# An LSTM with residual on one core: half products of x in two column quarters at 256 columns, and recurrent products that begin with the other two

## The chip, the cores and the metric

One core of a Trainium2 chip runs the whole program. The metric is the device time of one execution in microseconds. The kernel before was timed three times: 3061.52, 3061.62 and 3063.40 us, so its median is 3061.62 us.

## The reference

The input x has 32 sequences of 512 steps with 512 features; the start state h0 is given, the cell state starts at zero, and all numbers are 32-bit floats. The result is x plus the hidden states of an LSTM with 512 units. Cut to what is computed:

```python
xW = jnp.einsum('ntd,dg->ntg', x, Wx) + b          # Wx: 512 x 2048
def step(carry, xw_t):
    prev_h, prev_c = carry
    a = xw_t + prev_h @ Wh                         # Wh: 512 x 2048
    i = jax.nn.sigmoid(a[:, :Hd])
    f = jax.nn.sigmoid(a[:, Hd:2 * Hd])
    o = jax.nn.sigmoid(a[:, 2 * Hd:3 * Hd])
    g = jnp.tanh(a[:, 3 * Hd:])
    next_c = f * prev_c + i * g
    next_h = o * jnp.tanh(next_c)
    return ((next_h, next_c), next_h)
(_, _), hs = jax.lax.scan(step, (h0, c0), jnp.swapaxes(xW, 0, 1))
x = x + jnp.swapaxes(hs, 0, 1)
```

There are two kinds of product: x times Wx, which hangs on nothing but the inputs, and in each of the 512 steps the state times Wh, which hangs on the step before.

## The kernel before, in words

**Quarters.** Both kinds of product are issued as matmuls with 32 columns of weights, so that one matmul uses one quarter of the array's 128 columns. The quarter j of a matmul is named by the partitions that it writes, 32j to 32j+31. Four matmuls, one for each quarter, make one set.

**The recurrent product.** `h_part(t)` (L552) issues 16 matmuls: for each quarter k of the 512 units of the state, and for each column quarter j, 512 columns of `wh_sb`. They add into `bank_of(t)`, one of the two tiles `gbank`, which ScalarE filled before with x's part of that step (`seed_step`, L1035, a copy from `xw`). `cell(t)` (L565) then goes: sigmoids and tanh on ScalarE from `gbank` into `s` and `o`, products and a sum on VectorE (`prod`, `s`), a tanh on ScalarE (`tanh_c`), the product `hbuf`, and a transpose in two halves into `ht`, the weights of `h_part(t + 1)`. The first half of `ht` holds k = 0 and 1, the second k = 2 and 3.

**The products of x.** From step 18 to step 497 x times Wx is made in 15 groups of 32 steps by a scheme with fewer multiplications: 26 products for each group (a `slot` counts them through, 390 in all), and each of them out of seven of half the size (r = 1 to 7). One such (slot, r) is called an item here. An item is one set: four matmuls, one for each quarter, with 256 columns (`HW`) of the right operand in `vring` (L906). The left operand is a sum of blocks of x (`ubuf`), or a block in `xs` or `r`; the result goes to one of five `xbank` or to half of `bbank`. `evacuate` (L946) takes finished items to SBUF.

**Where they stand.** In the main loop `h_part(t)` is issued first, then `emit_matmuls(n)` (L868) issues n quarters of an item's work, then `cell(t)` is recorded. So between two recurrent products TensorE has items to do while the cell runs. `pos[0]` counts quarters of items. The count that is due by a step is worked out at L1588 as `R * 7 * 4 + (t + i - STREAM0) * R * 7 * 2 // GS * 2` with R = 26 and GS = 32, which grows by 22 or 24 a step, 22.75 in the mean. Where an item doesn't fit, a half of it is issued (`size = 2`): the half with q = 0 at the end of a step, and the half with q = 2 at the beginning of the next. In the kernel before, a half is 128 of the 256 columns in all four quarters.

Over 16 steps the formula gives, for where a step's items begin and end (0: whole, 2: in the middle of an item): five steps 0 to 2, three steps 2 to 2, five steps 2 to 0 and three steps 0 to 0. The steps 0 to 2 and 2 to 0 hold five and a half items, the other two kinds six. The main loop has 28 such rounds, so 140, 84, 140 and 84 steps.

**What sets the order.** The class `Plan` (L105) records every instruction and orders them by a model of their costs. TensorE's instructions keep the order in which they were recorded; those of the other queues are sorted by due times that are worked back from TensorE's. As everything is issued from one helper, all lines of the profile read L125, and groups are told apart by tiles.

Of the kernel before, what the change touches and what calls it, by code (L numbers as in the profile page):

```python
# [14 lines left out]
B = 32  # L15
T = 512
NJ = 4
# [5 lines left out]
HW = G * H  # L23
# [50 lines left out]
BIAS_OF = {  # L74
    2: "b1", 5: "b1-b0", 9: "-b2", 10: "b1", 12: "b0-b3", 13: "b0-b3", 14: "-b2", 15: "b3", 19: "b0-b1+b2", 21: "b3",
    22: "b0-b3",
}
# [3 lines left out]
RIGHT = {1: 0, 5: 1, 3: 2, 6: 3, 2: 4, 7: 5, 4: 6}  # L81
# [306 lines left out]
def kernel(  # L388
# [150 lines left out]
    def is_split(t):  # L539
        return t >= SPLIT  # L540

    def bank_of(t):
        return {2: xbank[3], 3: xbank[4], 4: xbank[0]}.get(t, gbank[t % 2])

    def half_of(t, i):
        if t == T - 1:
            return LAST[i][:, 0:HW]
        if is_split(t):
            return PAIRS[(t - SPLIT) % 2][i][:, 0:HW]
        return bank_of(t)[:, i * HW : (i + 1) * HW]  # L550

    def h_part(t):  # L552
        if is_split(t):
            order = [(i, k) for i, ks in ((0, (0, 1)), (1, (0,)), (0, (2, 3)), (1, (1, 2, 3))) for k in ks]
        else:
            order = [(None, k) for k in range(NJ)]
        for i, k in order:
            dst = bank_of(t) if i is None else half_of(t, i)
            m = wh_sb[:, k] if i is None else wh_sb[:, k, :, i * HW : (i + 1) * HW]
            for j in range(NJ):  # L560
                nc.tensor.matmul(
                    dst[j * B : (j + 1) * B], state["ht"][:, k], m[:, j], start=False, stop=True, skip_group_check=True
                )
# [104 lines left out]
    def group(g):  # L668
        if g not in groups:
            groups[g] = Group(g)  # L670
        return groups[g]
# [143 lines left out]
    def left_of(gr, s, r):  # L815
        b = u_block(gr, U_OF[s])
        return ubuf[:, gr.u[U_OF[s]], LEFT[r]] if b is None else b[:, 1 + LEFT[r]]

    def left_done(gr, s):
        u_used(gr, U_OF[s])  # L820
# [43 lines left out]
    pos = [0]  # L864
# [3 lines left out]
    def emit_matmuls(n):  # L868

        while n > 0 and pos[0] < 4 * len(items):  # L870
            i, q = divmod(pos[0], 4)
            row, slot, r = items[i]
            gr, s = group(slot // R), slot % R
            xb = xbank[slot % 5]
            if q == 0 and any(f in finished for f in needs(slot, r)):
                if wait_at_end[0]:
                    return
                evacuate()
            if r == 2:
                dst = bbank[:, slot % 2 * HW : (slot % 2 + 1) * HW]  # L880
            elif r in (5, 3):
                dst = xb[:, HW:W]
            else:
                dst = xb[:, 0:HW]
            start = q == 0 and (r == 2 or (r == 1 and s not in BIAS_OF))
            size = 4 if q == 0 and n >= 4 else 2
            cols = slice(q * HW // 4, (q + size) * HW // 4)
            for j in range(4):
                nc.tensor.matmul(
                    dst[j * B : (j + 1) * B, cols],  # L890
                    left_of(gr, s, r)[:, j * B : (j + 1) * B],
                    right_of(row, slot, RIGHT[r])[:, cols],
                    start=start,
                    stop=True,
                    skip_group_check=True,
                )
            pos[0] += size
            n -= size
            if pos[0] % 4 == 0:
                finished.append((slot, r))  # L900
                if r == 4:
                    left_done(gr, s)
                    if slot < HELD:
                        (free_u if slot == 1 else free_c).extend({1: (6, 7), 2: (V_OF[2],), 3: (V_OF[3],)}.get(slot, ()))

    def right_of(row, slot, k):  # L906
        if slot >= HELD:
            return vring[:, row % 3, k]
        return v_parts(V_OF[slot])[2] if k == 6 else v_parts(V_OF[slot])[k % 2][:, k // 2]

    def needs(slot, r):
        if r == 1:
            return ((slot - 5, 4),)
        if r == 2:
            return ((slot - 2, 2),)
        return {5: (), 6: ((slot, 5),), 3: ((slot, 5),), 7: ((slot, 3),), 4: ((slot, 7),)}[r]
# [29 lines left out]
    def evacuate():  # L946
        while wqueue and len(free_c) < sum(r == 5 for _, r in finished):
            w_op(True)
        for slot, r in finished:
            gr, s = group(slot // R), slot % R  # L950
            xb = xbank[slot % 5]
            if r == 5:
                gr.have[s, "c"] = take(free_c)
                t = buf_of(gr.have[s, "c"])
                nc.scalar.copy(t[:, 0:4:3], xb.rearrange("p (n c) -> p n c", n=2))
                continue
            if r in (1, 6):
                continue
            t = buf_of(gr.have[s, "c"])
            if r == 2:  # L960
                add(t[:, 0], bbank[:, slot % 2 * HW : (slot % 2 + 1) * HW], t[:, 0])
                room["dve"] -= cost_dve(256)
            elif r == 3:
                nc.scalar.copy(t[:, 1], xb[:, 0:HW])
                add(t[:, 1], xb[:, HW:W], t[:, 1])
                room["dve"] -= cost_dve(256)
            elif r == 7:
                add(t[:, 3], xb[:, 0:HW], t[:, 3])
                room["dve"] -= cost_dve(256)
            else:  # L970
                nc.scalar.copy(t[:, 2], xb[:, 0:HW])
                gr.have[s] = gr.have.pop((s, "c"))
                ready(gr, s)
        finished.clear()
# [92 lines left out]
    def v_parts(i):  # L1067
        if i < 8:
            return r1[:, i, 1:4], r2[:, i, 0:3], r2[:, i, 3]
        return split_parts(vroom[vt[i]])  # L1070
# [312 lines left out]
    with tc.manual_schedule():  # L1383
# [32 lines left out]
        for n in range(2):  # L1416
            for j in range(NJ):
# [4 lines left out]
                    start=True,  # L1422
# [44 lines left out]
        for t in range(T):  # L1467
            if t == 20:
                nc.flush()
            h_part(t)  # L1470
            for f in stores + kept_stores:
                f()
# [12 lines left out]
            if HEAD + 4 <= t < HEAD + 4 + 3 * len(V_DIRECT):  # L1485
                s, d = divmod(t - HEAD - 4, 3)
# [15 lines left out]
            if t < HEAD_STEPS:  # L1502
# [22 lines left out]
                for i, (kind, m, cs) in enumerate(chunks):  # L1525
# [16 lines left out]
                    else:  # L1542
# [22 lines left out]
                        if i == 0 and t + 1 in SEEDED and t + 1 != HEAD:  # L1565
                            seed_step(t + 1)
                        emit_matmuls(m)
                        room["dve"] += m * PROD / 4
                        if i == late_cell:
# [38 lines left out]
            if t in LATE:  # L1608
                late_loads.pop(0)()
            emit_matmuls(n)  # L1610
            load_v_ahead()
            if t == SPLIT - 1:
# [60 lines left out]
```

## Time and profile before

| what | value |
|---|---|
| median of three runs | 3061.62 us |
| the profiled execution: time | 3061.49 us |
| the profiled execution: span from first to last instruction | 3059.5 us |
| TensorE busy | 3050.5 us, 100% |
| VectorE busy | 2362.7 us, 77% |
| ScalarE busy | 1475.6 us, 48% |
| GpSimd busy | 227.7 us, 7% |
| DMA, mean | 247 GB/s |
| granted TensorE clock | 1.000 |

The profile's page is of one execution. Durations of matmuls in it are modelled ends of pipelined work, so one matmul lasts longer there than the distance to the next one that takes its place; distances between starts are the better measure. Each matmul of the program leaves two records: 466 recurrent products of 16 matmuls stand as 14,912 records.

### The profile page before, as it was taken

The numbers are of one execution on the slowest core, as the hardware profiler recorded it, in microseconds if no ns is written. First come the engines' busy times: TensorE is split into PE (matmuls) and PEld (weight loads), VectorE is DVE, ScalarE is ACT, GpSimd is POOL, SyncE is SP. The second block draws the span as 40 slices with busy tenths as digits, with TensorE's granted clock in tenths as the row PEclk, the third lists the DMA queues.
The fourth block names the chain that finished last, engine by engine and source line by source line (L and its number), as shares of the span: only waits on it lengthen the run. The fifth ranks groups of instructions, "written<-read, shape, count | busy, mean of one in ns | idle before, by whom it ended". The sixth has DMA issues, their size and how long they took to land.

```text
span 3059.5 us, 107940 instructions
## 1 busy us (share of the span) xinstructions
PE 3050.5 (100%) x43464; PEld 1586.6 (52%) x43464; DVE 2362.7 (77%) x6510; ACT 1475.6 (48%) x5499; POOL 227.7 (7%) x476
## 2 busy tenths in 40 slices
PE   9999999999999999999999999999999999999999
PEld 6644444444445555555555555555555555555666
DVE  8678787787877878788787877878778787787755
ACT  1345445454444544445445454454544545444454
POOL 1000000000000000000000000000000000000000
PEclk9999999999999999999999999999999999999999
DMA  9988887787877878778787787877877777788630
GB/s 329 326 285 279 267 254 258 239 260 242 262 249 242 263 236 269 240 245 270 229 277 234 247 266 237 272 237 244 265 244 254 251 251 259 244 263 269 210 95 19
DMA packets 323700, 755.75 MB, mean 247 GB/s; under 512 B 52352, under 2 KB 107904, under 8 KB 322688
## 3 DMA queue, kind: packets, MB, share of 16 engines
q1 hardware_dynamic: 323200, 748.84, 75.9%
q8 instruction: 343, 5.62, 0.8%
q14 instruction: 157, 1.29, 0.1%
HBM read 567.48 MB, written 184.30 MB: 246 GB/s over the span
## 4 chain that ended last, share of the span: by engine, by line
PE 98%; DVE 1%; DMA 1%; SPq 0%; ACT 0%; issue 0%; DVEq 0%
PE gbank L125 55%; PE xbank L125 37%; PE bbank L125 6%; DMA xwd<-xnat 0%; DVE ubuf L125 0%; SPq L125 0%; DMA xnat<-in_x_dram 0%; DMA seeds_at<-in_L_cond_b_dram 0%; DVE vring L125 0%; DVE prod L125 0%; DVE s L125 0%; DVE cbuf L125 0%; DVE hbuf L125 0%; DVE xbank L125 0%; ACT s L125 0%
## 5 line engine op out<-in xcount | busy, mean ns | idle before, releaser
L125 PE MATMUL gbank<-wh_sb,ht 128*32 128x512 f32 x14912 | 1694.7, 592 | 1.0 <-DVE ht L125 0.9
L125 PEld LDWEIGHTS gbank<-wh_sb,ht 128*32 128x32 f32 x14912 | 533.5, 110 | 825.6 <-issue 715.7
L125 ACT ACTIVATE s<-gbank 128x64 f32<-128x64 f32 (+2 forms) x1920 | 331.2, 257 | 1204.9 <-PE gbank L125 1203.5
L125 PE MATMUL xbank<-vring,ubuf 128*32 128x256 f32 (+1 forms) x13584 | 846.3, 368 | 0.0
L125 PEld LDWEIGHTS xbank<-vring,ubuf 128*32 128x32 f32 x13584 | 504.0, 110 | 314.2 <-issue 137.7
L125 DVE TENSOR_TENSOR prod<-s 128x128 f32<-128x128 f32 (+2 forms) x1093 | 296.9, 278 | 463.6 <-ACT s L125 458.9
L125 POOL TENSOR_TENSOR oc<-xnat,ht 128x128 f32<-128x128 f32 x469 | 222.6, 475 | 2606.5 <-DVE ht L125 1304.6
L125 ACT ACTIVATE tanh_c<-s 128x64 f32<-128x64 f32 (+1 forms) x921 | 237.2, 258 | 191.0 <-DVE s L125 188.6
L125 ACT COPY cbuf<-xbank 128x256 f32<-128x256 f32 (+1 forms) x694 | 288.2, 439 | 40.7 <-PE xbank L125 34.4
L125 ACT COPY gbank<-xw 128x512 f32<-128x512 f32 (+1 forms) x486 | 285.1, 589 | 1.8 <-DMA vring<-vdram 1.5
L125 DVE STREAM_TRANSPOSE ht<-hbuf 128x64 f32<-128x64 f32 (+1 forms) x921 | 226.9, 246 | 64.1 <-DVE hbuf L125 0.9
L125 DVE TENSOR_TENSOR s<-prod 128x64 f32<-128x64 f32 (+1 forms) x1007 | 227.4, 226 | 34.2
L125 DVE TENSOR_TENSOR cbuf<-xbank,cbuf 128x256 f32<-128x256 f32 x462 | 180.9, 409 | 48.3 <-ACT cbuf L125 42.9
L125 DVE TENSOR_TENSOR cbuf<-cbuf 128x1024 f32<-128x1024 f32 x172 | 209.6, 1223 | 1.2 <-ACT cbuf L125 0.5
L125 PE MATMUL xbank<-vring,r 128*32 128x256 f32 (+1 forms) x3216 | 206.6, 357 | 0.0
L125 PE MATMUL xbank<-vring,xs 128*32 128x256 f32 (+1 forms) x3120 | 200.6, 356 | 0.3 <-ACT xnat L125 0.3
L125 DVE TENSOR_TENSOR hbuf<-o,tanh_c 128x64 f32<-128x64 f32 (+1 forms) x921 | 190.3, 207 | 3.8 <-ACT tanh_c L125 3.1
L125 ACT COPY r<-xbank 128x256 f32<-128x256 f32 (+1 forms) x414 | 176.4, 439 | 16.0 <-PE xbank L125 12.9
L125 PE MATMUL bbank<-vring,ubuf 128*32 128x256 f32 (+1 forms) x2600 | 182.5, 342 | 0.0
L125 PEld LDWEIGHTS xbank<-vring,r 128*32 128x32 f32 x3216 | 117.4, 110 | 84.6 <-issue 47.5
L125 ACT ACTIVATE o<-gbank 128x128 f32<-128x128 f32 (+1 forms) x508 | 154.7, 305 | 0.0
L125 PEld LDWEIGHTS xbank<-vring,xs 128*32 128x32 f32 x3120 | 115.0, 110 | 63.9 <-issue 23.5
(173 smaller groups left out, 2290.3 us busy)
## 6 DMA issues: line engine op xcount, KB each, us to landing
vring<-vdram SPq DMA_DIRECT2D x310, 896.0 KB, 5.8
xw<-xwd SPq DMA_DIRECT2D x1920, 64.0 KB, 4.5
xwd<-cbuf SPq DMA_DIRECT2D x140, 512.0 KB, 4.6
xwd<-r SPq DMA_DIRECT2D x83, 512.0 KB, 4.9
out_dram<-oc SPq DMA_DIRECT2D x255, 128.0 KB, 3.7
xnat<-in_x_dram SPq DMA_DIRECT2D x62, 512.0 KB, 5.3
xs<-in_x_grouped_dram SPq DMA_DIRECT2D x45, 512.0 KB, 4.8
vring<-vdram SPq DMA_DIRECT2D x33, 512.0 KB, 5.1
```

What stands on the lines that cost most here:

```text
L125: self.plan.add(self.name, op, lambda: call(*args, **kw), out, rest)
```

## The change

A half of an item no longer takes 128 columns in four quarters. With q = 0 it takes the whole 256 columns in quarters 0 and 1, and with q = 2 in quarters 2 and 3. `h_part` reads where the items stand (`turn = pos[0] % 4`, 0 or 2), and issues its quarters, for each k, in the order 2, 3, 0, 1 when the step before ended in the middle of an item. As each half now covers columns that the other doesn't touch in its own partitions, `start` no longer hangs on q.

```diff
@@ h_part
+        turn = pos[0] % 4
         for i, k in order:
             dst = bank_of(t) if i is None else half_of(t, i)
             m = wh_sb[:, k] if i is None else wh_sb[:, k, :, i * HW : (i + 1) * HW]
-            for j in range(NJ):
+            for j in [*range(turn, NJ), *range(turn)]:
                 nc.tensor.matmul(
                     dst[j * B : (j + 1) * B], state["ht"][:, k], m[:, j], start=False, stop=True, skip_group_check=True
                 )
@@ emit_matmuls
-            start = q == 0 and (r == 2 or (r == 1 and s not in BIAS_OF))
+            start = r == 2 or (r == 1 and s not in BIAS_OF)
             size = 4 if q == 0 and n >= 4 else 2
-            cols = slice(q * HW // 4, (q + size) * HW // 4)
-            for j in range(4):
+            for j in range(q, q + size):
                 nc.tensor.matmul(
-                    dst[j * B : (j + 1) * B, cols],
+                    dst[j * B : (j + 1) * B],
                     left_of(gr, s, r)[:, j * B : (j + 1) * B],
-                    right_of(row, slot, RIGHT[r])[:, cols],
+                    right_of(row, slot, RIGHT[r]),
                     start=start,
                     stop=True,
                     skip_group_check=True,
```

How TensorE's instructions stand at a place in the middle of the program is shown next, where a step ends with half an item. In these rows `xbank_66` to `xbank_70` are the five banks of items, `gbank_72` and `gbank_73` the two banks of the recurrent product with `ht_95` and `ht_96` as its weights; 32x256 is the shape that one matmul writes, and xN counts equal matmuls that follow each other. Before:

```order
L125 MATMUL bbank<-vring,r_74 32x256 x4
L125 MATMUL xbank_69<-vring,r_74 32x128 x4
L125 MATMUL gbank_72<-wh_sb,ht_96 32x512 x16
L125 MATMUL xbank_69<-vring,r_74 32x128 x4
L125 MATMUL xbank_68<-vring,ubuf 32x256 x8
```

The same place of the change:

```order
L125 MATMUL bbank<-vring,r_74 32x256 x4
L125 MATMUL xbank_69<-vring,r_74 32x256 x2
L125 MATMUL gbank_72<-wh_sb,ht_96 32x512 x16
L125 MATMUL xbank_69<-vring,r_74 32x256 x2
L125 MATMUL xbank_68<-vring,ubuf 32x256 x8
```

The halves stand where they stood, one on each side of the recurrent product, with two matmuls each in place of four. That the 16 of the recurrent product now begin with quarter 2 can't be seen in these rows.

The second place is on TensorE too, directly behind the first: a step ends with half an item, the next begins with its other half and ends whole. Before:

```order
L125 MATMUL xbank_66<-vring,ubuf 32x256 x4
L125 MATMUL bbank<-vring,ubuf 32x128 x4
L125 MATMUL gbank_73<-wh_sb,ht_95 32x512 x16
L125 MATMUL bbank<-vring,ubuf 32x128 x4
L125 MATMUL xbank_70<-vring,r_74 32x256 x4
L125 MATMUL xbank_69<-vring,r_74 32x256 x8
L125 MATMUL xbank_68<-vring,ubuf 32x256 x8
L125 MATMUL gbank_72<-wh_sb,ht_96 32x512 x16
```

And of the change:

```order
L125 MATMUL xbank_66<-vring,ubuf 32x256 x4
L125 MATMUL bbank<-vring,ubuf 32x256 x2
L125 MATMUL gbank_73<-wh_sb,ht_95 32x512 x16
L125 MATMUL bbank<-vring,ubuf 32x256 x2
L125 MATMUL xbank_70<-vring,r_74 32x256 x4
L125 MATMUL xbank_69<-vring,r_74 32x256 x8
L125 MATMUL xbank_68<-vring,ubuf 32x256 x8
L125 MATMUL gbank_72<-wh_sb,ht_96 32x512 x16
```

Again only the two halves differ. The rows of VectorE, ScalarE, GpSimd and SyncE are the same in both programs, in the same order.

## The prediction, as it was made before the changed kernel was run

> **What bounds the kernel now.** First the page: which engine fills the span, and which chain ended last.
>
> ```profile
> span 3059.5 us, 107940 instructions
> PE 3050.5 (100%) x43464; PEld 1586.6 (52%) x43464; DVE 2362.7 (77%) x6510; ACT 1475.6 (48%) x5499; POOL 227.7 (7%) x476
> PE 98%; DVE 1%; DMA 1%; SPq 0%; ACT 0%; issue 0%; DVEq 0%
> ```
>
> TensorE is without work for 9 us, and 98% of the last chain is its own. The next view, TensorE's waits, says how little of this is the recurrence:
>
> ```profile
> PE gbank L125 <- DVE ht L125: 0.9, 1, 0.9
> PE xbank L125 <- DVE ht L125: 0.4, 1, 0.4
> ```
>
> A reader would conclude that only work on the array counts. But how far is the recurrence from showing up? For that I read TensorE's timeline over three steps in the middle (start, duration, tiles, count of records):
>
> ```profile
> 1479.91 0.64 PE L125 MATMUL xbank<-vring,r 128*32 128x256 f32 x8
> 1480.35 1.07 PE L125 MATMUL xbank<-vring,ubuf 128*32 128x256 f32 x16
> 1481.21 0.64 PE L125 MATMUL xbank<-vring,r 128*32 128x256 f32 x8
> 1481.64 0.64 PE L125 MATMUL bbank<-vring,r 128*32 128x256 f32 x8
> 1482.07 0.43 PE L125 MATMUL xbank<-vring,r 128*32 128x128 f32 x8
> 1482.29 3.64 PE L125 MATMUL gbank<-wh_sb,ht 128*32 128x512 f32 x32
> 1485.72 0.43 PE L125 MATMUL xbank<-vring,r 128*32 128x128 f32 x8
> 1485.94 1.07 PE L125 MATMUL xbank<-vring,ubuf 128*32 128x256 f32 x16
> 1486.81 1.07 PE L125 MATMUL xbank<-vring,r 128*32 128x256 f32 x16
> 1487.67 0.64 PE L125 MATMUL xbank<-vring,ubuf 128*32 128x256 f32 x8
> 1488.10 0.43 PE L125 MATMUL bbank<-vring,ubuf 128*32 128x128 f32 x8
> 1488.32 3.64 PE L125 MATMUL gbank<-wh_sb,ht 128*32 128x512 f32 x32
> 1491.75 0.43 PE L125 MATMUL bbank<-vring,ubuf 128*32 128x128 f32 x8
> 1491.97 1.50 PE L125 MATMUL xbank<-vring,r 128*32 128x256 f32 x24
> 1493.27 1.07 PE L125 MATMUL xbank<-vring,ubuf 128*32 128x256 f32 x16
> 1494.13 1.45 PE L125 MATMUL gbank<-wh_sb,ht 128*32 128x512 f32 x9
> ```
>
> By starts: five items (1479.91 to 1482.07) take 2.16 us, 0.432 each; a half of 128 columns in four quarters 0.22 (the four of them that stand here agree to the last digit; I use 0.218, a little over half an item's 0.216); a recurrent product 3.43 (1482.29 to 1485.72). These three steps are one of each kind: 0 to 2, 2 to 2, 2 to 0. Between the end of one recurrent product and the start of the next lie 2.38, 2.60 and 2.38 us of items. I call that stretch the cover: the cell must be done within it.
>
> How long does the cell need? One step, at the end of the loop, has only five items, and no half:
>
> ```profile
> 2852.86 0.64 PE L125 MATMUL bbank<-vring,ubuf 128*32 128x256 f32 x8
> 2853.30 1.07 PE L125 MATMUL xbank<-vring,ubuf 128*32 128x256 f32 x16
> 2854.16 0.64 PE L125 MATMUL bbank<-vring,ubuf 128*32 128x256 f32 x8
> 2854.59 0.64 PE L125 MATMUL xbank<-vring,ubuf 128*32 128x256 f32 x8
> 2855.21 0.64 PE L125 MATMUL gbank<-wh_sb,ht 128*32 128x512 f32 x4
> 2854.82 0.24 DVE L125 STREAM_TRANSPOSE ht<-hbuf 128x64 f32<-128x64 f32 x1
> ```
>
> Its items end at 2854.59 + 0.43 = 2855.02, the first half of `ht` is there at 2854.82 + 0.24 = 2855.06, and the product starts at 2855.21, 0.15 after that and **2.35 us** after the step's first item. (The busy column hides this wait, since the modelled end of the last item is 2855.23.) In the ordinary steps the transpose ends just as late:
>
> ```profile
> 1481.87 0.24 DVE L125 STREAM_TRANSPOSE ht<-hbuf 128x64 f32<-128x64 f32 x1
> 1493.70 0.25 DVE L125 STREAM_TRANSPOSE ht<-hbuf 128x64 f32<-128x64 f32 x1
> ```
>
> 1482.11 is 2.20 after 1479.91, and 1493.95 is 2.20 after 1491.75; with 0.15 for the way to TensorE both give 2.35 again, of a cover of 2.38. So the recurrence is 0.03 us from binding in every step with five and a half items. Whatever shortens the cover or lengthens the recurrent product, from its first start to its last end, shows at once.
>
> **The change, part by part.** *Work on the array.* A step's halves keep their sum: two quarters for 0.432 us are as much as four for 0.218. The records of 128 columns in the loop are these:
>
> ```profile
> L125 PE MATMUL xbank<-vring,ubuf 128*32 128x128 f32 x1344 | 70.9, 273 | 0.0
> L125 PE MATMUL bbank<-vring,ubuf 128*32 128x128 f32 x896 | 47.2, 273 | 0.0
> L125 PE MATMUL xbank<-vring,r 128*32 128x128 f32 x672 | 35.4, 273 | 0.0
> L125 PE MATMUL xbank<-vring,xs 128*32 128x128 f32 x672 | 35.4, 273 | 0.0
> ```
>
> They are 3584, sixteen for each split item, so 224 items, which agrees with 140 + 84 steps that end in a half. Each split item costs 2 x 0.218 where a whole one costs 0.432: the change saves about 0.005 us for each, 1.1 us in all. That is the whole gain there can be on a full array.
>
> *Do quarters run apart?* No row shows two quarters busy with one product while two work on another. What bears on it is the beginning of a recurrent product, read in two windows of different length:
>
> ```profile
> 1482.29 0.64 PE L125 MATMUL gbank<-wh_sb,ht 128*32 128x512 f32 x4
> 1482.29 1.02 PE L125 MATMUL gbank<-wh_sb,ht 128*32 128x512 f32 x5
> ```
>
> One record lasts 0.59, as the group's row below has it. Four cover 0.64, so the fourth starts 0.05 after the first; five cover 1.02, so the fifth starts 0.43 after the first and 0.38 after the fourth, whose place is taken for 0.43 (eight sets in 3.43). The fifth doesn't wait for the fourth to be through: each quarter seems to go on when it is free itself. If they are tied together, a half costs up to 0.43 alone; if they are free, nothing. I take free, which is nearest to that row, and keep the other end for the rivals.
>
> ```profile
> L125 PE MATMUL gbank<-wh_sb,ht 128*32 128x512 f32 x14912 | 1694.7, 592 | 1.0 <-DVE ht L125 0.9
> ```
>
> *The step 0 to 2.* Counted from the end of the recurrent product before: all quarters have five items until 2.16. Quarters 0 and 1 then do their half until 2.59. Quarters 2 and 3 are free at 2.16, but the state isn't there before 2.35: they idle for 0.19, and lead by 0.24 and not by 0.43. Quarters 0 and 1 begin at 2.59 and end at 2.59 + 3.43 = 6.02. The cell needs all of `gbank`, so the next one starts at 6.02, where before it was 2.38 + 3.43 = 5.81: **+0.213** (2.590 against 2.377). What is queued on TensorE behind the wait for `ht` is the recurrent product itself and all that follows; the halves of quarters 0 and 1 stand ahead of it.
>
> *The step 2 to 2.* Quarters 2 and 3 end their part 0.24 early and do their half until 0.19 after the others; then five items, the half on 0 and 1 until 2.59, and `ht` at 2.35 again. 2.59 + 3.43 = 6.02 against 2.595 + 3.43: −0.005.
>
> *The step 2 to 0.* Quarters 2 and 3 end their items at 0.19 + 2.16 = 2.35, quarters 0 and 1 at 2.16. All need `ht`: the product starts when the cell is done, not at 2.377. Here quarters 0 and 1 idle for what the others lost before. For the cell I take 2.34, a little under 2.35: the last matmul of a product that began with quarter 2 is that of quarter 1, a few hundredths lower in the stagger of 0.05. That gives −0.037. The steps 0 to 0 are as they were, with 2.59 of items.
>
> *Sum.* 140 x (0.213 − 0.037) − 84 x 0.005 = 24.6 − 0.4 = **24.2 us**. Against the profiled execution's own time (3061.5, of which 3059.5 is span; the median of the runs is 3061.6) this is 3085.7; I say 3085. If the cell needs 2.30 where it is quickest, the sum is 140 x 0.136 − 0.4 = 18.6, so 3080; if the new order costs 0.06 more on that path, 140 x 0.236 − 0.4 = 32.6, so 3094.
>
> *The other queues.* VectorE, ScalarE, GpSimd and SyncE keep their instructions in order. Their waits for finished items come at the same distance from the cell's start or up to 0.04 earlier (a half begun before is through at 0.19, not 0.22). That moves nothing late; DMA and the `xw` copies get more time in a longer step.
>
> **The rivals.** *Starts keep the program's order.* Then the first pass of quarter 0 can't start before the second pass of quarter 2, which stands ahead of it in each k if a matmul's two records follow each other: 2.34 + 0.43 = 2.77 in place of 2.59. A step 0 to 2 ends at 6.20 (+0.39), a step 2 to 2 too (+0.17), a step 2 to 0 gains 0.04: 140 x 0.35 + 84 x 0.17 = 63 us, 3125. Against it: four records start within 0.05 of each other and a quarter's second pass comes 0.43 later, so later matmuls do pass an earlier one's second record today. The Trainium skill, in "TensorE: Matmul & The Clock Gate", Part 3 on what overlaps and what doesn't, has it that matmuls start and end strictly in program order; this rival is what that rule would do here, and the four starts within 0.05 us speak against its strict form.
>
> *A half is done alone.* If quarters 2 and 3 wait for the half and the half for the whole product, each of the 448 halves costs 0.432 and not 0.218: +96 us, 3157. `ht` is then never late, since the cover is 2.59. The fifth record of the window above speaks against it.
>
> *Not slower: the state is early enough.* The lead of quarters 2 and 3 costs nothing if the cell's way is 2.16 or shorter, so that they start at once, end 0.43 early, and do their half while the others end; the next cell would still start from quarters 0 and 1, and the loss of 0.213 would have to come back whole in the step 2 to 0 (2.377 − 0.213 = 2.164). From that point down the change gains its 1.1 us: 3060.4. The step at 2852.86 speaks against it: with 2.16 of cover it waited until 2.35. The same time comes out if the array works on two quarters at a time with both passes of a matmul, so that a half of two matmuls takes 0.216 as it is; the trace doesn't name the quarter of a record.
>
> **How the numbers follow.** Free quarters with a cell of 2.30 to 2.40: 0.80, predicted 3085, own range 3078 to 3095. Program order 0.06; a half alone 0.04; no loss 0.08; a gain for a reason I don't see 0.02. The range 3074 to 3105 holds the first case and the part of the second where the order binds only sometimes, with a margin of some us below for a cell that is quicker than its bound. A measurement of this kernel tells 0.2%, some 6 us, from no change. Faster by that 0.02, the same 0.08, slower 0.90.
>
> **What would show it.** In the timeline of the changed kernel, a recurrent product behind a half lasts 3.67 from its first start to the next step's first item on quarter 0, not 3.43, and the first starts lie 2.35 behind that point in all steps with a half. The records of 128 columns in the loop are gone, 1792 of 256 columns come in their place. TensorE stays at 100% busy, as one pair of quarters always works: the loss is not visible as idle time there, only as idle time of ScalarE before `s<-gbank`. With a half done alone the product keeps 3.43 and a half's row shows 0.43. I am wrong if the product's length doesn't change and the halves still take 0.22, or if the cell's path itself gets longer, which the transposes would show.

## The result, and the profile after

The changed kernel takes 3080.97 us (median of 6 runs, 3080.63 to 3083.21) where the kernel before took 3061.57 us beside it: 1.0064 times as long, 95% interval 1.0051 to 1.0077. That is 19.4 us more. Forecast were 24 us more, 3085, in a range of 3074 to 3105.

The first lines of the page of the changed kernel are these:

```profile
span 3078.9 us, 104356 instructions
PE 3070.3 (100%) x41672; PEld 2057.7 (67%) x41672; DVE 2362.7 (77%) x6510; ACT 1476.3 (48%) x5499; POOL 229.1 (7%) x476
```

TensorE is as full as it was: 8.6 us without a record, where there were 9. From this view alone nobody would find the loss. TensorE has 1792 fewer matmul records and 19.8 us more busy time, because a record of one pair of quarters counts as busy while the other pair stands idle. The loss is visible on ScalarE, in the group of the cell's first sigmoids, first before and then after (busy us, mean ns, idle us before them and what ended it):

```profile
L125 ACT ACTIVATE s<-gbank 128x128 f32<-128x128 f32 x960 | 269.3, 281 | 1167.0 <-PE gbank L125 1165.5
```

```profile
L125 ACT ACTIVATE s<-gbank 128x128 f32<-128x128 f32 x960 | 269.4, 281 | 1185.1 <-PE gbank L125 1183.6
```

The sigmoids themselves take the same time; ScalarE waits 18.1 us longer for `gbank`.

The timeline of TensorE shows where. These rows of the changed kernel are the same three steps that the prediction showed of before (0 to 2, 2 to 2, 2 to 0):

```profile
1489.01 0.66 PE L125 MATMUL xbank<-vring,r 128*32 128x256 f32 x8
...
1491.17 0.41 PE L125 MATMUL xbank<-vring,r 128*32 128x256 f32 x2
1491.36 0.62 PE L125 MATMUL gbank<-wh_sb,ht 128*32 128x512 f32 x2
1491.38 0.41 PE L125 MATMUL xbank<-vring,r 128*32 128x256 f32 x2
1491.60 3.63 PE L125 MATMUL gbank<-wh_sb,ht 128*32 128x512 f32 x30
1494.79 0.59 PE L125 MATMUL xbank<-vring,r 128*32 128x256 f32 x3
1495.03 0.38 PE L125 MATMUL xbank<-vring,ubuf 128*32 128x256 f32 x1
...
1497.38 0.59 PE L125 MATMUL gbank<-wh_sb,ht 128*32 128x512 f32 x1
...
1501.06 0.38 PE L125 MATMUL xbank<-vring,r 128*32 128x256 f32 x1
...
1503.36 3.67 PE L125 MATMUL gbank<-wh_sb,ht 128*32 128x512 f32 x32
1506.79 0.67 PE L125 MATMUL xbank<-vring,r 128*32 128x256 f32 x8
```

Read it by pairs of records. Each matmul's two records are its two passes. The trace doesn't name the quarter of a record; I take it from the program and from which quarters are free. At 1491.17 and 1491.38 quarters 0 and 1 do the two passes of their half. At 1491.36, between them, two records of the recurrent product start: quarters 2 and 3, 2.35 us after the step's first item at 1489.01. Quarters 0 and 1 follow at 1491.60, 0.24 later. The other half comes at 1494.79 on quarters 2 and 3, while quarters 0 and 1 still work on the product; they go on to the next item at 1495.03. The recurrent product now takes 3.67 us from its first start to that point. The step 0 to 2 takes 6.02 us (1489.01 to 1495.03), the step 2 to 2 6.03 (to 1501.06), the step 2 to 0 5.73 (to 1506.79); before they took 5.81, 6.03 and 5.81.

These rows are from the middle of the loop. In the steps up to about 140 the same loss lies otherwise: by the records' own nanoseconds one pair of quarters is 0.15 to 0.20 us ahead in the products behind a half, and still 0.07 to 0.13 ahead in the others. The two steps 0 to 2 and 2 to 0 together take as long there as later.

### The profile page after: what moved, and what is told of

It is laid out like the page before. It is cut to its first block, busy times and chain, and to the rows that moved or that the text cites. A ratio compares the mean times of both kernels' runs of the same rounds, so it can differ in the third digit from the quotient of the medians.

```text
span 3078.9 us, 104356 instructions
## 1 busy us (share of the span) xinstructions
PE 3070.3 (100%) x41672; PEld 2057.7 (67%) x41672; DVE 2362.7 (77%) x6510; ACT 1476.3 (48%) x5499; POOL 229.1 (7%) x476
## 4 chain that ended last, share of the span: by engine, by line
PE 98%; DMA 1%; DVE 1%; SPq 0%; ACT 0%; issue 0%; DVEq 0%
PE gbank L125 55%; PE xbank L125 37%; PE bbank L125 6%; DMA bias_full<-in_L_cond_b_dram 0%; DMA r<-in_L_cond_Wx_dram 0%; DVE ubuf L125 0%; SPq L125 0%; DMA seeds_at<-in_L_cond_b_dram 0%; DVE vring L125 0%; DVE prod L125 0%; DVE xs L125 0%; DVE cbuf L125 0%; DVE s L125 0%; DVE hbuf L125 0%; DVE gbank L125 0%
## 5 line engine op out<-in xcount | busy, mean ns | idle before, releaser
L125 PE MATMUL gbank<-wh_sb,ht 128*32 128x512 f32 x14912 | 1753.3, 593 | 1.6 <-DVE ht L125 1.6
L125 PEld LDWEIGHTS gbank<-wh_sb,ht 128*32 128x32 f32 x14912 | 817.5, 110 | 588.1 <-issue 319.3
L125 PE MATMUL xbank<-vring,ubuf 128*32 128x256 f32 x12912 | 946.2, 379 | 0.0
L125 PEld LDWEIGHTS xbank<-vring,ubuf 128*32 128x32 f32 x12912 | 641.5, 110 | 201.2 <-issue 74.7
L125 PE MATMUL xbank<-vring,r 128*32 128x256 f32 x2880 | 243.9, 379 | 0.0
L125 PE MATMUL xbank<-vring,xs 128*32 128x256 f32 x2784 | 240.2, 379 | 0.0
L125 PE MATMUL bbank<-vring,ubuf 128*32 128x256 f32 x2152 | 230.5, 379 | 0.0
L125 PEld LDWEIGHTS xbank<-vring,r 128*32 128x32 f32 x2880 | 149.4, 110 | 54.6 <-issue 19.9
L125 PEld LDWEIGHTS xbank<-vring,xs 128*32 128x32 f32 x2784 | 147.5, 110 | 34.3 <-issue 1.3
```

Of the source, the lines that this page charges most:

```text
L125: self.plan.add(self.name, op, lambda: call(*args, **kw), out, rest)
```

## The experiments

**The order of the quarters alone taken back.** The changed kernel, but every recurrent product is issued in the order 0, 1, 2, 3:

```diff
-        turn = pos[0] % 4
...
-            for j in [*range(turn, NJ), *range(turn)]:
+            for j in range(NJ):
```

> The changed kernel, but the recurrent product always issues its quarters in the order 0, 1, 2, 3. Theory (quarters run free, and matmuls of idle quarters pass those that wait): quarters 2 and 3 still begin at 2.35 us behind the step's first item, the time stays within 4 us of the changed kernel's 3081. Rival (what stands ahead in the program holds what is behind it): quarters 2 and 3 wait with 0 and 1 until 2.59, have no lead, and do their half 0.43 late; then each of the 140 pairs of steps 0 to 2 and 2 to 0 costs 0.21 twice, and the time is about 3120.

Measured: 3086.83 us, 1.0084 times before (1.0069 to 1.0099), 5.9 us more than the changed kernel. The rival's 3120 is far off; the 4 us that the theory allowed are exceeded too. TensorE's timeline of this run at a step 0 to 2:

```profile
1491.68 0.65 PE L125 MATMUL xbank<-vring,r 128*32 128x256 f32 x8
...
1493.84 0.41 PE L125 MATMUL xbank<-vring,r 128*32 128x256 f32 x2
1494.04 0.62 PE L125 MATMUL gbank<-wh_sb,ht 128*32 128x512 f32 x2
1494.06 0.41 PE L125 MATMUL xbank<-vring,r 128*32 128x256 f32 x2
1494.27 3.63 PE L125 MATMUL gbank<-wh_sb,ht 128*32 128x512 f32 x30
```

Quarters 2 and 3 begin the product at 1494.04, 2.36 after the step's first item, although the program has the matmuls of quarters 0 and 1 ahead of them, and those wait for their half until 1494.27. So later matmuls do pass waiting ones of another quarter, and the lead doesn't need the new order. What the order changes is the end. With 0, 1, 2, 3 the last matmul in the program is quarter 3's, which is through early, and ScalarE still starts later than in the changed kernel. The next rows are ScalarE's first sigmoid in a step 2 to 0, in this run (first item on the quarters 0 and 1 at 1503.73) and in the changed kernel (at 1501.06):

```profile
1504.00 0.68 ACT L125 ACTIVATE s<-gbank 128x128 f32<-128x128 f32 x4 [2.21 <-PE gbank L125]
```

```profile
1501.29 0.68 ACT L125 ACTIVATE s<-gbank 128x128 f32<-128x128 f32 x4 [2.20 <-PE gbank L125]
```

0.27 against 0.23. Over 136 steps of this run that begin with a half and end whole, counted from the records' own nanoseconds, the median from the end of the last pass (its start and 0.429 us, the distance between two passes in one quarter) to the sigmoid is 0.233 us, in the changed kernel 0.200, and the product starts 2.348 after the first item, in place of 2.315. Times 140 that is 4.6 of the 5.9 us. The rest isn't accounted for step by step.

**Whole items only.** The kernel before, with items never split; eleven of 16 steps get six, five get five:

```diff
-                max(0, min(R * 7 * 4 + (t + i - STREAM0) * R * 7 * 2 // GS * 2, 4 * len(items)) - pos[0]) for i in (1, 2)
+                max(0, min(R * 7 * 4 + (t + i - STREAM0) * R * 7 // GS * 4, 4 * len(items)) - pos[0]) for i in (1, 2)
```

> The kernel before with whole items only: eleven of 16 steps get six, five get five, and no item is split. Theory (the loss of the change is a cover of five items, 2.16 us, where the cell needs 2.31 to 2.35): 140 steps with five items wait 0.16 to 0.19 each for the state, less 1.1 us for the halves that are gone: 22 to 26 us above before, 3084 to 3088, as much as the change lost or a little more. Rival (the loss comes from work in two quarters at a time, not from the cover): 3060 to 3062.

Measured: 3087.75 us, 1.0084 times before (1.0067 to 1.0101), 26.3 us more than before: the upper end of what the theory gave. A step with five items, from TensorE's and VectorE's timelines of this run:

```profile
1434.11 1.07 PE L125 MATMUL xbank<-vring,ubuf 128*32 128x256 f32 x16
1434.98 1.07 PE L125 MATMUL xbank<-vring,xs 128*32 128x256 f32 x16
1435.84 0.64 PE L125 MATMUL xbank<-vring,ubuf 128*32 128x256 f32 x8
1436.45 3.64 PE L125 MATMUL gbank<-wh_sb,ht 128*32 128x512 f32 x32
1436.06 0.25 DVE L125 STREAM_TRANSPOSE ht<-hbuf 128x64 f32<-128x64 f32 x1
```

The items end at 1435.84 + 0.43 = 1436.27, `ht` is there at 1436.31, the product starts at 1436.45, 2.34 after the first item. With four quarters always together, and no halves at all, the same kind of loss is there, and 6.8 us more of it than in the changed kernel. In the median of its steps with five items the product starts 2.347 us after the first item, where it starts 2.315 after it in the changed kernel; times 140 that is 4.5 of the 6.8. The rest isn't accounted for. So a half in two quarters does little more for the cover than no half: what is left to it is the quicker end above.

**A shorter cell, first attempt.** In the changed kernel and in the one before, the tanh of the cell state is left out from step 17 to the split steps:

```diff
-            for u in part:
+            for u in part if is_split(t) else ():
                 nc.scalar.activation(tanh[:, HALVES[u]], nxt[:, u, 3], AF.Tanh)
             for u in part:
-                nc.vector.tensor_mul(hbuf[:, HALVES[u]], o[:, u], tanh[:, HALVES[u]])
+                c_out = tanh[:, HALVES[u]] if is_split(t) else nxt[:, u, 3]
+                nc.vector.tensor_mul(hbuf[:, HALVES[u]], o[:, u], c_out)
```

> The changed kernel with a shorter cell: from step 17 to the split steps the tanh of the cell state is left out, and hbuf is o times the cell state itself. The cell needs some 0.4 us less, about 1.9 us, under the 2.16 of five items. Theory (the loss is the wait for the state): the loss of 19 us vanishes, 3058 to 3062, and the recurrent product behind a half starts on quarters 2 and 3 at 2.16, not 2.35. Rival (two quarters at a time cost TensorE time of their own): 3078 to 3082 still.

> The kernel before with the same shorter cell, the tanh of the cell state left out from step 17 to the split steps: the pair to the changed kernel with it. Both theories: bound by the array, 3057 to 3062; the changed kernel with the short cell should lie 1 us below it by the theory, 17 to 20 us above it by the rival.

Measured: 3080.85 us for the changed kernel (1.0064 times before, 1.0049 to 1.0079), 3062.29 for the other (1.0002, 0.9992 to 1.0011). By the numbers written down this is the rival's outcome. But the cell hadn't become shorter. VectorE's timeline of the changed kernel in a step 2 to 0, with the tanh:

```profile
1502.50 0.23 DVE L125 TENSOR_TENSOR s<-prod 128x64 f32<-128x64 f32 x1
1502.64 0.22 DVE L125 TENSOR_TENSOR hbuf<-o,tanh_c 128x64 f32<-128x64 f32 x1
1502.97 0.24 DVE L125 STREAM_TRANSPOSE ht<-hbuf 128x64 f32<-128x64 f32 x1
```

And without it, in this run, in a step 0 to 2. The lag between the pairs lies the other way round there, so that it is again the later pair's first item that counts, which begins with these weight loads:

```profile
1491.68 0.14 PEld L125 LDWEIGHTS xbank<-vring,r 128*32 128x32 f32 x2
```

```profile
1492.80 0.28 DVE L125 TENSOR_TENSOR prod<-s 128x128 f32<-128x128 f32 x1
1493.12 0.23 DVE L125 TENSOR_TENSOR s<-prod 128x64 f32<-128x64 f32 x1
1493.27 0.22 DVE L125 TENSOR_TENSOR hbuf<-o,s 128x64 f32<-128x64 f32 x1
1493.59 0.25 DVE L125 STREAM_TRANSPOSE ht<-hbuf 128x64 f32<-128x64 f32 x1
```

`hbuf` follows the second half's sum in both, and the transpose ends 2.15 us after the later pair's first item with the tanh (1503.21 − 1501.06) and 2.16 without (1493.84 − 1491.68). The tanh of the first half lay beside VectorE's work for the second half. So this pair tested nothing; the claim in its expectation, that the cell would need 0.4 us less, was wrong.

**A shorter cell, second attempt.** In both kernels, in the same steps, the tanh is left out, and for the second half of the units the cell state too, so that two VectorE instructions go from in front of the first transpose:

```diff
-            for u in part:
+            for u in part if is_split(t) else (0,):
...
-            for u in part:
+            for u in part if is_split(t) else ():
                 nc.scalar.activation(tanh[:, HALVES[u]], nxt[:, u, 3], AF.Tanh)
             for u in part:
-                nc.vector.tensor_mul(hbuf[:, HALVES[u]], o[:, u], tanh[:, HALVES[u]])
+                c_out = tanh[:, HALVES[u]] if is_split(t) else (nxt[:, 0, 3], s[:, 1, 2])[u]
+                nc.vector.tensor_mul(hbuf[:, HALVES[u]], o[:, u], c_out)
```

> The changed kernel with a cell that is really shorter: from step 17 to the split steps the tanh of the cell state is left out, and for the second half of the units the cell state too (no product with it, no sum; hbuf is o times tanh of g there). Two VectorE instructions of 284 and 225 ns go from in front of the first transpose, so the first half of ht should be there about 1.85 us after the step's first item, and the product could start at 2.0. Theory (the loss is the wait for the state): with the state before 2.16 nothing waits, quarters 2 and 3 start at 2.16 with a lead of 0.43, and the time is 3058 to 3062. Rival (two quarters at a time cost TensorE time of their own): 3079 to 3082.

> The kernel before with the same cut cell (the same parts left out): its pair. Both theories: bound by the array, 3058 to 3062. The changed kernel with it should lie 1 us below by the theory, 17 to 20 above by the rival.

Measured: 3059.21 us for the changed kernel (10 runs, 3058.63 to 3059.49; 0.9991 times before, 0.9981 to 1.0000), and 3060.41 for the other (10 runs, 3059.58 to 3061.16; 0.9996, 0.9987 to 1.0006). The 19 us are gone, and the changed kernel lies 1.2 us below its pair; the two sets of runs don't overlap. TensorE's timeline of the first:

```profile
1440.34 0.60 PE L125 MATMUL gbank<-wh_sb,ht 128*32 128x512 f32 x2
1440.37 0.38 PE L125 MATMUL xbank<-vring,ubuf 128*32 128x256 f32 x1
1440.55 3.63 PE L125 MATMUL gbank<-wh_sb,ht 128*32 128x512 f32 x30
...
1446.14 0.59 PE L125 MATMUL gbank<-wh_sb,ht 128*32 128x512 f32 x1
...
1451.95 0.60 PE L125 MATMUL gbank<-wh_sb,ht 128*32 128x512 f32 x2
```

The lead is still there (1440.34 and 1440.55), and the steps take 5.80 and 5.81 us, as in the kernel before. That the wait is gone can be read beside VectorE's first transpose of the second of these steps; the first row's start is the leading pair's first item:

```profile
1443.77 1.67 PE L125 MATMUL xbank<-vring,ubuf 128*32 128x256 f32 x23
```

```profile
1445.63 0.24 DVE L125 STREAM_TRANSPOSE ht<-hbuf 128x64 f32<-128x64 f32 x1
```

The transpose ends at 1445.87, 2.10 after the leading pair's first item and 1.89 after the later pair's (0.21 behind it). The product starts at 1446.14, which is five items (2.16) after the later pair's first item and 0.27 after the transpose; a product that waits for the transpose starts 0.15 after it.

The lead of 0.43 that was expected isn't there in these rows: one pair of quarters is 0.21 ahead behind a half, and the other pair 0.21 ahead elsewhere. Earlier in the same run it is, 0.41 behind a half (709.87 and 710.28) and none in the other products:

```profile
704.26 3.65 PE L125 MATMUL gbank<-wh_sb,ht 128*32 128x512 f32 x32
...
709.87 0.63 PE L125 MATMUL gbank<-wh_sb,ht 128*32 128x512 f32 x2
...
710.28 3.60 PE L125 MATMUL gbank<-wh_sb,ht 128*32 128x512 f32 x30
...
715.88 3.65 PE L125 MATMUL gbank<-wh_sb,ht 128*32 128x512 f32 x32
```

What moves the lead during the loop isn't shown. The two steps together take the same either way: 11.62 from 704.26 to 715.88, 11.61 from 1440.34 to 1451.95, and twice 5.81 in the kernel before. Two pairs of quarters working apart cost TensorE nothing that these runs can tell.

**The new order alone.** The kernel before, halves in four quarters, with `turn` and the order 2, 3, 0, 1:

```diff
+        turn = pos[0] % 4
...
-            for j in range(NJ):
+            for j in [*range(turn, NJ), *range(turn)]:
```

> The kernel before with its halves in all four quarters, and only the order 2, 3, 0, 1 of the recurrent product behind a half. Theory (quarters are full either way, and ends are signalled in the program's order, some 17 ns apart): ScalarE's first sigmoid starts 0.24 us after the last end in these steps, not 0.22, the cover of 2.38 still just holds, and the time is within 2 us of before. Rival (the new order alone is what costs or gains): more than 4 us from before.

Measured: 3061.14 us, 1.0000 times before (0.9990 to 1.0009). By the records' nanoseconds ScalarE starts 0.243 after the last end in the steps with the new order, and 0.220 in the others, as the theory had it. The order neither costs nor gains where all quarters end together.

## Why the prediction was right, point by point

- *The cover is the bound.* It was said that the recurrence, hidden with 0.03 us to spare, would set the time wherever the cover falls to five items. Shown: the second cut cell takes the wait away and the loss with it, and the kernel with whole items has the same kind of loss with no halves at all.
- *Quarters run free.* This was taken from one reading, the fifth record that starts 0.38 us after the fourth. It is shown by the rows at 1491.36 and 1494.79 and by the cut cell, where running apart costs nothing.
- *The step 0 to 2 and the step 2 to 2.* 6.02 and 6.02 were forecast, 6.02 and 6.03 stand in the rows. That is the loop from about step 140 on. Before that the pair 0 to 2 and 2 to 0 shares its loss otherwise (5.89 and 5.87 in the steps 20 to 60), with the same sum. The prediction had one way of sharing for the whole loop; the time didn't hang on that.
- *The step 2 to 0* was mis-sized. The cell was put at 2.34 us behind the first item; it is 2.315 in the median of the steps that begin with a half and end whole. The pair was to cost 0.176 and costs 0.146: the mean lengths of the two steps in the trace are 5.959 and 5.810 us, 11.769 together, where they were 5.813 and 5.811. Times 140 that is 20.4 us, less 0.4 for the steps 2 to 2, and 19.9 in the loop as a whole. The term was a little under by intention ("a few hundredths lower in the stagger"); what was missed is that the signal itself comes 0.02 sooner, 0.200 us after the last end and not 0.220.
- *The gain on the array.* 1.1 us were forecast; the medians of the pair with the cut cell differ by 1.2. In their two traces the loop itself differs by 0.5 only, so the agreement is in part luck.
- *The rivals.* The program's order (3125) is refuted at the start of a product by the run with the order 0, 1, 2, 3. The Trainium skill says, in "TensorE: Matmul & The Clock Gate", Part 3 on what overlaps and what doesn't, that matmuls start in program order; the rows of that run at 1494.04 and 1494.27 say otherwise for these 32-bit matmuls in different quarters, and the measurement decides. A half done alone (3157) is refuted by the two halves' rows. The state being early enough (3060) is right as a mechanism, but the kernel's cell lies on the other side of its limit: with the cell cut to 2.04 us (1.89 and the 0.15 to TensorE), below 2.16, it is what happens. The other way to the same time, a half done in 0.216, is refuted by the rows at 1491.17 and 1491.38: the second passes start 0.21 after the first, so the half holds its two quarters for 0.43.
- *What would show it.* The 1792 records, the 100% of TensorE and ScalarE's longer wait all came as written. The 3.67 us from first start to next item came from about step 140 on. The first starts 2.35 behind that point were to stand in all steps with a half: they do in the steps 0 to 2 and 2 to 2 of the rows (1489.01 to 1491.36 and 1495.03 to 1497.38), and in the step 2 to 0 it is 2.30 (1501.06 to 1503.36).

## What to carry to other kernels

Where a recurrence is hidden by filling work, the slack of that cover is a number to measure before the filling is moved: here it was 0.03 us in 5.8, and an arrangement of equal total work lost 19 us. Letting one part of the array begin earlier helps only if its input is there earlier; if it isn't, the part that begins late sets the end, and the chain grows by the lag. And before an instruction is called part of a critical path, look whether its engine or its neighbour's queue is what the next one waits for: a tanh of 0.26 us was worth nothing.

## What the runs showed of the hardware that had not been expected

TensorE's quarters can start out of the program's order; when their ends are told looks as if it followed that order. The time from the end of the last pass to ScalarE's first sigmoid was 0.220 us in the kernel before, 0.200 in the changed one, 0.233 with the order 0, 1, 2, 3 and a lead, 0.243 with the order 2, 3, 0, 1 and no lead. These are medians of the records' own nanoseconds. In the traces' semaphore records TensorE's signal comes 0.198, 0.178, 0.211 and 0.220 us after that end, and ScalarE starts 0.022 or 0.023 after the signal every time: the difference arises before the signal, not on ScalarE. All four fit one rule, which is worked out from these runs and not seen directly: the ends of four matmuls are reported one after another in the program's order, at least 17 ns apart, and ScalarE starts 0.200 after the last report. In the kernel before, the four ends lie at 0, 34, 41 and 48 ns, so the reports at 0, 34, 51 and 68, 20 after the last end; in the changed kernel the last two in the program lie 34 apart and report at once; with 0, 1, 2, 3 the late quarter 1 is followed by two reports, 34 ns; with 2, 3, 0, 1 without a lead the value 0.24 was written down before that run. Two places that the rule wasn't made from fit too. In the kernel before, in the steps up to about 139, the ends lie at 0, 7, 13 and 20, so the last report is due 31 after the last end, and ScalarE starts 0.230 after it. In the changed kernel with the cut cell, in its steps 126 to 283, the last two ends of a product behind a half lie 7 apart (0, 34, 221 and 228), so the last report is due 10 after, and ScalarE starts 0.210 after.

A busy TensorE row can hide idle quarters: with one pair waiting and the other working, the page shows 100%.
